# A graph network's front: edge windows gathered in node order, ranking before the table, places kept on chip

## The chip, the cores and the metric

The kernel runs on one NeuronCore of a Trainium2 chip. The metric is the device time of one execution in microseconds, the median over several runs. A separate execution is profiled; its times count from the start of its span.

The engines are TensorE (PE, with its weight loads PEld), VectorE (DVE), ScalarE (ACT), GpSimd (POOL) and SyncE (SP). Each works through its own instructions in order. SP and ACT issue plain transfers; POOL issues the indirect ones, which gather or scatter rows by an index list.

## The reference

The graph has 1250 nodes with 768 features and 20,000 edges, sorted by destination. Two layers follow each other, each behind a layer norm and ReLU and each with a residual. The first consists of two attention convolutions, with 8 heads and then 1:

```python
fs = (x @ Ws + bs).reshape(-1, H, D)
fd = (x @ Wd + bd).reshape(-1, H, D)
e = leaky_relu(fs[src] + fd[dst], 0.2)
logits = einsum('ehd,hd->eh', e, attn)
alpha = softmax of logits over the edges of each dst
out = elu(segment_sum(alpha[:, :, None] * fs[src], dst))
```

The second is a relational convolution, where each of 34 edge types has a 768x768 matrix that multiplies the mean of a node's neighbours of that type, and then a plain graph convolution.

## The kernel before, in words

All inputs and outputs are float32. The nodes are ranked by degree and cut into ten tiles of 128, so that each tile has a fixed number of edge slots (33, 22, 20, ... 11: `CAPS`, 179 in all). One slot of a tile is one "row" of the attention: one indirect gather of 128 source rows.

`fast_front` prepares this.

- It loads the edges and the nodes, normalizes the nodes (stored as `h0_d`) and transposes them to `hT` on TensorE.
- `sources(j)` (L802 on) multiplies node tile j by the first layer's source weights: two accumulations of twelve products and a bias product, two copies on ACT, and one store to the table `fs_d` on SP. There are ten such tiles.
- The ranking counts on VectorE how many 32-edge rows start below a node (L768), gathers one row of 32 destinations for each node (`got`, L775) and so finds where its edges begin (`first`, L827) and its degree. A product with a shifted identity (`sh_ps`, L830) brings each partition the first edge of the next. The degrees are broadcast as keys by eight products (L857, L858), and ten counts (L863) give the ranks. Ten scatters (L878) write records of four integers (node, first edge, degree) to the DRAM table `rank_d` at the node's rank, and one load (`rk`, L899) brings them back in rank order.
- The lists follow in rank order. `win_d` holds each edge packed as type * 2048 + source, in overlapping windows of 64. Ten gathers (`win`, L910) fetch each node's window, and five steps of three VectorE instructions (L924 to L927) shift it by its offset. `f.ell` is the result; `f.srci` (L929) is the source index that the attention gathers by.
- `pairs()` (called later, from `prepare_lists`) gives each edge a place in the lists of the second layer: counts of each type (L957, L959), masks (L965), prefix products on TensorE (L968 to L977), then the turns (L1025 to L1028), the arithmetic on the prefix sums (L984 to L1014), the picks (L1022, L1023) and the places (L1066). A product (`fl_ps`, L1061) raises a flag where the graph does not fit.

`attention` then runs over the rows. `front` gathers a row into a ring of 24 buffers and computes its logits in three VectorE instructions (L1205, L1210, L1211). `back` scales it by the softmax on ACT (L1263) and sums on TensorE (L1265), which frees its buffer. Tiles are cut in chunks: the first tile's are 16 and 17 rows long, and the back of one chunk runs beside the front of the next. `negated1` gathers a tile's own nodes (`h0`) and multiplies them for the destination term `nfd` (L1409). `finish1` ends a tile with two more matrix products and scatters its row of the second table.

Behind the gathers of the first attention, `list_edges` issues the scatters that write each edge to its place in `pair_d` (L1149), one for each row of edges, 179 in all. A `rate` of 0.9 scatters is due for each gathered row from row 20 of the first tile; at the last row 60 more are due, which empties the list. They need the places and the filled `pair_d` (L1363).

The order of the work: each engine's order is fixed by a planner that traces the program, estimates times, and takes among the instructions that are ready the one that stands first in the program. `tc.issue_after(x)` puts what a block issues on x's engine behind x. In the kernel before this sets TensorE's order: tile 0, the shift product, tile 1, the key products, tile 2; the other seven tiles follow in program order. Buffers of pools that are closed are reused by later pools, which wait for their last readers: the attention's gather buffers lie where the front's `hT` and weights were.

Of the kernel before, what the change touches and what calls it, by code (L numbers as in the profile page):

```python
# [10 lines left out]
F32 = mybir.dt.float32  # L11
# [614 lines left out]
def fast_front(ctx, tc, f, x, src, dst, edge_type, W1s, b1s, W1d, b1d, attn1, attno, W_rel):  # L626
# [34 lines left out]
    rank_d = dram.tile([NP, 4], I32, name="f_rank_d")  # L661
# [9 lines left out]
    f.ell = keepp.tile([P, NT, S0], I32, name="f_ell")  # L671
# [3 lines left out]
    f.place_d = dram.tile([P, NT * S0], I32, name="f_place_d")  # L675
    f.w1d = keepp.tile([P, KC, D], F32, name="f_w1d")

    with ExitStack() as front:
# [141 lines left out]
        last = sources(0)  # L820
# [8 lines left out]
        with tc.issue_after(last.ins):  # L829
            last = nc.tensor.matmul(sh_ps[:, 0:1], shift, first[:, 0:1], start=True, stop=True)  # L830
        with tc.issue_after(last.ins):
            last = sources(1)
# [3 lines left out]


# [14 lines left out]
        with tc.issue_after(last.ins):  # L852
            for g in range(2):
                wide = ps_m.tile([P, 2, 512], F32, name="wide", tag="ag").rearrange("p a b -> p (a b)")
                for lo, hi in ((0, 512), (512, N // 2)):
                    at = slice(g * (N // 2) + lo, g * (N // 2) + hi)
                    nc.tensor.matmul(wide[:, lo:hi], ones16[:EP], flat2[:, at], start=True, stop=False)  # L857
                    last = nc.tensor.matmul(wide[:, lo:hi], big16[:EP], flat[:, at], start=False, stop=True)  # L858
                nc.scalar.copy(keys[:, g * (N // 2):(g + 1) * (N // 2)], wide[:, :N // 2])
# [7 lines left out]
        rec = prep.tile([P, NT, 4], I32, name="rec")  # L867
        nc.vector.memset(rec, 0)
        nc.vector.tensor_copy(rec[:, :, 0], node)
        nc.vector.tensor_copy(rec[:, :, 1], first[:, :NT])  # L870
        nc.vector.tensor_copy(rec[:, :, 2], deg)

        past = prep.tile([NP - N, 4], I32, name="past")
# [10 lines left out]
        with tc.issue_after(last_keys.ins):  # L884
            sources(2)


        packed = prep.tile([EP, EC], I32, name="packed")
        nc.vector.scalar_tensor_tensor(packed, ev[:, 2, :], 2048.0, ev[:, 0, :], op0=ALU.mult, op1=ALU.add)
        zrow = prep.tile([1, RW], I32, name="zrow")  # L890
        nc.vector.memset(zrow, 0)
        pk = packed.rearrange("p (r c) -> p r c", c=RW)
        nc.scalar.dma_start(win_d[1:NR + 1, :RW].rearrange("(p r) c -> p r c", p=EP), pk)
        nc.scalar.dma_start(win_d[0:NR, RW:].rearrange("(p r) c -> p r c", p=EP), pk)
        nc.scalar.dma_start(win_d[NR:NR + 1, RW:], zrow)


        rk = prep.tile([P, NT, 4], I32, name="rk")
# [3 lines left out]
        nc.vector.tensor_copy(f.degf, rk[:, :, 2])  # L902
        arow = prep.tile([P, NT], I32, name="arow")
        nc.vector.tensor_scalar(arow, rk[:, :, 1], 5, None, op0=ALU.arith_shift_right)
        nc.vector.tensor_scalar(arow, arow, float(NR - 1), 1.0, op0=ALU.min, op1=ALU.add)
        offs = prep.tile([P, NT], I32, name="offs")
        nc.vector.tensor_scalar(offs, rk[:, :, 1], RW - 1, None, op0=ALU.bitwise_and)
        win = prep.tile([P, NT, WIN], I32, name="win")
        for k in range(NT):
            nc.gpsimd.indirect_dma_start(  # L910
                out=win[:, k, :], out_offset=None, in_=win_d[:, :],
                in_offset=bass.IndirectOffsetOnAxis(ap=arow[:, k:k + 1], axis=0))
        wf = prep.tile([P, NT, WIN], F32, name="wf")
        nc.vector.tensor_copy(wf, win)
        bits = prep.tile([P, 5, NT], F32, name="bits")
        for i in range(5):
            bi = prep.tile([P, NT], I32, name="bi", tag="bi", bufs=2)
            nc.vector.tensor_scalar(bi, offs, i, 1, op0=ALU.arith_shift_right, op1=ALU.bitwise_and)
            nc.vector.tensor_copy(bits[:, i, :], bi)
        for i in (4, 3, 2, 1, 0):  # L920
            b = 1 << i
            L = S0 + b - 1
            df = prep.tile([P, NT, S0 + 15], F32, name="df", tag="df")
            nc.vector.tensor_sub(df[:, :, :L], wf[:, :, b:b + L], wf[:, :, :L])  # L924
            nc.vector.tensor_tensor(df[:, :, :L], df[:, :, :L],
                                    bits[:, i, :, None].to_broadcast([P, NT, L]), op=ALU.mult)
            nc.vector.tensor_add(wf[:, :, :L], wf[:, :, :L], df[:, :, :L])  # L927
        nc.vector.tensor_copy(f.ell, wf[:, :, :S0])
        nc.vector.tensor_scalar(f.srci, f.ell, 2047, None, op0=ALU.bitwise_and)  # L929
# [5 lines left out]
        def pairs():  # L935
# [13 lines left out]
            typ = pp.tile([P, NT, S0], I32, name="typ")  # L949
            nc.vector.tensor_scalar(typ, f.ell, 11, None, op0=ALU.arith_shift_right)  # L950
            tv = pp.tile([P, NT, S0], F16, name="tv")
            nc.vector.scalar_tensor_tensor(tv, pad, 100.0, typ, op0=ALU.mult, op1=ALU.add)
# [101 lines left out]
            pl_i = pp.tile([P, NT, S0], I32, name="pl_i")  # L1054
# [11 lines left out]
            nc.vector.scalar_tensor_tensor(pl_i, pad, float(P * COLS), pl, op0=ALU.mult, op1=ALU.add)  # L1066
            nc.sync.dma_start(f.place_d[:, :], pl_i.rearrange("p k s -> p (k s)"))

        for j in range(3, NT):
            sources(j)  # L1070
# [53 lines left out]
def fast_rest(ctx, tc, f, x, src, dst, edge_type, W1s, b1s, W1d, b1d, attn1, ln1_w, ln1_b,  # L1124
# [44 lines left out]
    def attention(H, table, negated, attn_e, first, loads, finish, rate, rest):  # L1169
# [21 lines left out]
        def front(c, i):  # L1191

            t, s = c.t, c.first + i
            fs = pool.tile([P, RW], F32, name="fs", tag="fs", bufs=ring)
            row = gather(fs[:, :W], table[:, :], f.srci[:, t.k, s:s + 1])
            fs = fs[:, :W].rearrange("p (h e) -> p h e", h=H)
            if s >= CHUNK or t.k:
                list_edges(row, rate)
            if t.k == NT - 1 and s == t.S - 1:
                list_edges(row, rest)  # L1200
            if t.lg is None:
                lg = pool.tile([P, S0 * f.H], F32, name="lg", tag="lg", bufs=2)
                t.lg = lg[:, :S0 * H].rearrange("p (s h) -> p s h", h=H)
            z = rows_tile("z", 2)
            nc.vector.tensor_tensor(z, fs, t.nfd, op=ALU.max)  # L1205
            if H == 1:
                nc.vector.scalar_tensor_tensor(z[:, 0, :], z[:, 0, :], 1.0, attn_e[:, 0, :], op0=ALU.mult,  # L1207
                                               op1=ALU.mult, accum_out=t.lg[:, s, :])
            else:
                nc.vector.tensor_mul(z, z, attn_e)  # L1210
                nc.vector.tensor_reduce(t.lg[:, s, :], z, axis=AX.X, op=ALU.add)  # L1211
            c.rows.append(fs)
# [133 lines left out]
    def prepare_lists():  # L1346
# [22 lines left out]
        f.place = rp.tile([P, NT, S0], I32, name="place")  # L1369
        nc.sync.dma_start(f.place, f.place_d.rearrange("p (k s) -> p k s", k=NT))  # L1370
# [19 lines left out]
    with ExitStack() as one:  # L1390
# [46 lines left out]
        attention(H, f.fs_d, negated1, f.attn_1, prepare_lists, loads1, finish1, 0.9, 60)  # L1437
# [277 lines left out]
```

## Time and profile before

| | us |
|---|---|
| median of 3 runs | 2816.5 (2815.39 to 2821.32) |
| the profiled execution | 2810.31 |
| its span | 2808.5 |
| TensorE busy | 2396.5 (85%) |
| VectorE busy | 1615.1 (58%) |
| GpSimd busy | 1471.1 (52%) |
| ScalarE busy | 852.6 (30%) |

The front lasts until about 147 us (table complete). The first attention's gathers begin at 152 and its tail ends at 902. The second attention begins there, and from about 1260 TensorE's products for the 34 types dominate, until 2567. The last part sums over neighbours.

A busy time is an average over stages; what counts in a stage is the wait that ends last there. In a line of groups, the count stands after the x, then the busy time and the mean length in ns, then the idle time before the group and what ended it. In a line of the timeline the start and the length come first, and idle time before it stands in brackets with its releaser.

### The profile page before, as it was taken

To read this page: it belongs to the slowest core of one execution; us is meant where nothing else is said; L and a number is where in the kernel's file an instruction comes from. 1 tells how busy PE (TensorE), PEld (TensorE's weight loads), DVE (VectorE), ACT (ScalarE), POOL (GpSimd) and SP (SyncE) were. 2 spreads that over 40 slices of the span, in tenths; PEclk is the share of its full clock that TensorE was granted. 3 is DMA by queue.
4 is the path that set the end of the run, shared out by engine and by line. 5 is a ranking of instruction groups with operands and counts; after the bars stand their busy time and mean duration, and the time that the engine had idled before them with its cause. 6 is when DMAs were issued, how large, how long until landed. Compare 5 with 4: busy or idle time off the path is not lost. (4 is left out here: it accounts for less than half of the span.)

```text
span 2808.5 us, 24226 instructions
## 1 busy us (share of the span) xinstructions
PE 2396.5 (85%) x7859; PEld 1395.3 (50%) x7859; DVE 1615.1 (58%) x2382; ACT 852.6 (30%) x2340; POOL 1471.1 (52%) x1039
## 2 busy tenths in 40 slices
PE   6942684789898386889599999999999999997998
PEld 3521252445454243545366666666666666664455
DVE  5579979898994999999463433343333333310000
ACT  3003774776762122333212122212212212221000
POOL 1332877787884776776374555455455544421000
PEclk9976997999999698999799999999999999999999
DMA  6144443444431766675477777777677777665211
GB/s 213 46 157 156 134 132 91 125 145 134 133 97 53 277 206 189 212 220 169 169 196 214 191 185 197 184 187 186 181 201 186 184 201 198 174 147 136 75 45 51
DMA packets 130769, 447.82 MB, mean 159 GB/s; under 512 B 25016, under 2 KB 27601, under 8 KB 130634
## 3 DMA queue, kind: packets, MB, share of 16 engines
q0 software_dynamic: 77792, 305.26, 41.7%
q1 hardware_dynamic: 48041, 133.96, 13.4%
q10 hardware_dynamic: 4800, 6.96, 0.7%
q8 instruction: 65, 1.06, 0.2%
q14 instruction: 71, 0.57, 0.1%
HBM read 357.08 MB, written 89.11 MB: 159 GB/s over the span
## 5 line engine op out<-in xcount | busy, mean ns | idle before, releaser
L1114 PE MATMUL ps<-wrel,mT 128*128 128x384 f32 x3336 | 1099.4, 486 | 1.2 <-DMA wrel<-in_L_gnn_W_rel_dram 1.2
L1114 PEld LDWEIGHTS ps<-wrel,mT 128*128 128x128 f32 x3336 | 623.2, 190 | 407.4 <-issue 1.5
L1145 POOL DMA_INDIRECT g<-r_h_d,lists x241 | 365.9, 1518 | 474.1 <-DVE g L1566 302.3
L1265 PE MATMUL ag<-fs,identf 128*128 128x384 f32 x716 | 290.2, 539 | 173.2 <-ACT fs L1263 163.4
L1263 ACT ACTIVATE fs<-fs,lg 128x96 f32<-128x96 f32 x1376 | 370.6, 362 | 2.4 <-issue 1.9
L1566 DVE TENSOR_TENSOR g<-g,g 128x768 f32<-128x768 f32 x68 | 64.6, 949 | 526.4 <-DMA g<-r_h_d,lists 464.7
L1205 DVE TENSOR_TENSOR z<-fs,nfd 128x776 f32<-128x776 f32 (+1 forms) x358 | 344.0, 976 | 39.6 <-DMA fs<-f_fs_d,srci 22.6
L1255 PE MATMUL ag<-fs,dg 128*128 128x384 f32 x716 | 252.3, 514 | 86.2 <-ACT dg L1253 45.9
L1145 POOL DMA_INDIRECT fs<-f_fs_d,srci x179 | 245.9, 1374 | 103.1 <-issue 47.2
L1592 POOL DMA_INDIRECT r_h_d<-y,lists x139 | 227.3, 1635 | 133.1 <-ACT y L1591 65.8
L1149 POOL DMA_INDIRECT r_pair_d<-rec,place x179 | 240.9, 1346 | 101.3 <-DVE lg L1211 48.6
L1265 PEld LDWEIGHTS ag<-fs,identf 128*128 128x128 f32 x716 | 135.2, 204 | 315.7 <-ACT fs L1263 247.5
L1145 POOL DMA_INDIRECT fs<-r_fs_d,srci x179 | 242.5, 1355 | 82.6 <-PE ag L1255 35.5
L1506 DVE SCALAR_TENSOR_TENSOR arow<-node,from_f,arow 128x1250 f16<-128x1250 f16 x179 | 270.7, 1514 | 3.7
L1255 PEld LDWEIGHTS ag<-fs,dg 128*128 128x128 f32 x716 | 142.9, 202 | 190.8 <-ACT dg L1253 91.1
L1591 ACT COPY y<-ps 128x768 f32<-128x768 f32 x71 | 56.8, 799 | 482.0 <-PE ps L1114 482.0
L1589 ACT ACTIVATE y<-ps,rcnt 128x768 f32<-128x768 f32 x68 | 61.3, 902 | 444.4 <-PE ps L1114 444.4
L1207 DVE SCALAR_TENSOR_TENSOR z<-z,attn_o 128x769 f32<-128x769 f32 x179 | 180.2, 1027 | 0.0
L1210 DVE TENSOR_TENSOR z<-z,attn 128x776 f32<-128x776 f32 x179 | 168.3, 954 | 0.1
L1211 DVE TENSOR_REDUCE lg<-z 128x8 f32<-128x776 f32 x179 | 167.9, 950 | 0.1
L1647 DVE COPY gT<-hb 128x512 f32<-128x512 f32 (+1 forms) x9 | 5.4, 603 | 250.0 <-ACT gT L1646 250.0
L1643 PE MATMUL hb<-adj,h 125*128 125x512 f32 (+1 forms) x360 | 130.9, 526 | 14.6 <-DMA h<-r_h_d 14.6
(274 smaller groups left out, 2269.7 us busy)
## 6 DMA issues: line engine op xcount, KB each, us to landing
wrel<-in_L_gnn_W_rel_dram SPq DMA_DIRECT2D x37, 2304.0 KB
g<-r_h_d,lists POOLq DMA_INDIRECT x241
r_nfd_d<-fd SPq DMA_DIRECT2D x10, 384.0 KB
nfd<-r_nfd_d SPq DMA_DIRECT2D x10, 384.0 KB
r_x_d<-xb SPq DMA_DIRECT2D x10, 384.0 KB
x1r<-r_x_d SPq DMA_DIRECT2D x10, 384.0 KB
f_fs_d<-o_s SPq DMA_DIRECT2D x9, 388.0 KB
x<-in_x_dram SPq DMA_DIRECT2D x9, 384.0 KB
```

Source lines behind the costliest of these rows:

```text
L1114: last = nc.tensor.matmul(ps[:n, half, :f.HW], hT[:, k, j * P:j * P + n], w[:, k, cols], start=(k == 0), stop=(k == f.KC - 1 and not bias))
L1145: return nc.gpsimd.indirect_dma_start(out=to, out_offset=None, in_=table, in_offset=bass.IndirectOffsetOnAxis(ap=idx, axis=0))
L1149: s = nc.gpsimd.indirect_dma_start(out=table, out_offset=bass.IndirectOffsetOnAxis(ap=idx, axis=0), in_=rows, in_offset=None, **kw)
L1205: nc.vector.tensor_tensor(z, fs, t.nfd, op=ALU.max)
L1207: nc.vector.scalar_tensor_tensor(z[:, 0, :], z[:, 0, :], 1.0, attn_e[:, 0, :], op0=ALU.mult, op1=ALU.mult, accum_out=t.lg[:, s, :])
L1210: nc.vector.tensor_mul(z, z, attn_e)
L1211: nc.vector.tensor_reduce(t.lg[:, s, :], z, axis=AX.X, op=ALU.add)
L1255: nc.tensor.matmul(c.ps[:, half, :HW], dg, fs[:, 0, half * HW:(half + 1) * HW], start=begin, stop=end)
L1263: nc.scalar.activation(fs[:, h, :HD], fs[:, h, :HD], AF.Copy, scale=t.lg[:, s, h:h + 1])
L1265: nc.tensor.matmul(c.ps[:, half, :HW].rearrange("p (h d) -> p h d", d=HD), f.identf, fs[:, half * H // 2:(half + 1) * H // 2, :HD], start= ...
L1506: nc.vector.scalar_tensor_tensor(a, node16, from_f[:, k, s:s + 1], a, op0=ALU.is_equal, op1=ALU.add)
L1592: s = nc.gpsimd.indirect_dma_start(out=h1_d[:, :], out_offset=bass.IndirectOffsetOnAxis(ap=j.node, axis=0), in_=y, in_offset=None, compute ...
```

## The change

The edge windows are gathered and shifted in node order, before the ranks exist, and the scatter to ranks carries the finished slots. Its records have 35 integers (node, degree, 33 slots) instead of four. After the reload only the two fields are separated, source and type; the type is kept (`f.typ`) and the packed slots (`f.ell`) are not.

All ten table tiles follow the key products on TensorE; the shift product and the key products wait for no table tile.

The places are computed into a buffer that stays, where before they were stored to DRAM and loaded again.

The edge scatters are due differently: none before row 23 of the first tile, 32 (40 times the rate) at that row, then 0.8 a row; what remains is due at the last row as before.

```diff
-    rank_d = dram.tile([NP, 4], I32, name="f_rank_d")
+    rank_d = dram.tile([NP, 2 + S0], I32, name="f_rank_d")
...
-    f.ell = keepp.tile([P, NT, S0], I32, name="f_ell")
+    f.typ = keepp.tile([P, NT, S0], I32, name="f_typ")
...
-    f.place_d = dram.tile([P, NT * S0], I32, name="f_place_d")
+    f.place = keepp.tile([P, NT, S0], I32, name="place")
...
-        last = sources(0)
...
-        with tc.issue_after(last.ins):
-            last = nc.tensor.matmul(sh_ps[:, 0:1], shift, first[:, 0:1], start=True, stop=True)
-        with tc.issue_after(last.ins):
-            last = sources(1)
+        nc.tensor.matmul(sh_ps[:, 0:1], shift, first[:, 0:1], start=True, stop=True)
...
+        packed = prep.tile([EP, EC], I32, name="packed")
+        nc.vector.scalar_tensor_tensor(packed, ev[:, 2, :], 2048.0, ev[:, 0, :], op0=ALU.mult, op1=ALU.add)
...
+        nc.scalar.dma_start(win_d[1:NR + 1, :RW].rearrange("(p r) c -> p r c", p=EP), pk)
+        nc.scalar.dma_start(win_d[0:NR, RW:].rearrange("(p r) c -> p r c", p=EP), pk)
...
+        nc.vector.tensor_copy(begin, first[:, :NT])
+        nc.vector.tensor_scalar(arow, begin, 5, None, op0=ALU.arith_shift_right)
...
+        for j in range(NT):
+            nc.gpsimd.indirect_dma_start(
+                out=win[:EP, j, :], out_offset=None, in_=win_d[:, :],
+                in_offset=bass.IndirectOffsetOnAxis(ap=arow[:EP, j:j + 1], axis=0))
...
-        with tc.issue_after(last.ins):
-            for g in range(2):
...
+        for g in range(2):
+            wide = ps_m.tile([P, 2, 512], F32, name="wide", tag="ag").rearrange("p a b -> p (a b)")
+            for lo, hi in ((0, 512), (512, N // 2)):
...
+        wf = prep.tile([P, NT, WIN], F32, name="wf")
+        nc.vector.tensor_copy(wf[:EP], win[:EP])
...
+        for i in (4, 3, 2, 1, 0):
+            b = 1 << i
+            L = S0 + b - 1
...
+            nc.vector.tensor_sub(df[:EP, :, :L], wf[:EP, :, b:b + L], wf[:EP, :, :L])
+            nc.vector.tensor_tensor(df[:EP, :, :L], df[:EP, :, :L],
+                                    bits[:EP, i, :, None].to_broadcast([EP, NT, L]), op=ALU.mult)
+            nc.vector.tensor_add(wf[:EP, :, :L], wf[:EP, :, :L], df[:EP, :, :L])
+        rec = prep.tile([P, NT, 2 + S0], I32, name="rec")
         nc.vector.tensor_copy(rec[:, :, 0], node)
-        nc.vector.tensor_copy(rec[:, :, 1], first[:, :NT])
-        nc.vector.tensor_copy(rec[:, :, 2], deg)
+        nc.vector.tensor_copy(rec[:, :, 1], deg)
+        nc.vector.tensor_copy(rec[:EP, :, 2:], wf[:EP, :, :S0])
...
         with tc.issue_after(last_keys.ins):
-            sources(2)
+            sources(0)
...
-        for k in range(NT):
-            nc.gpsimd.indirect_dma_start(
-                out=win[:, k, :], out_offset=None, in_=win_d[:, :],
-                in_offset=bass.IndirectOffsetOnAxis(ap=arow[:, k:k + 1], axis=0))
...
-        nc.vector.tensor_copy(f.ell, wf[:, :, :S0])
-        nc.vector.tensor_scalar(f.srci, f.ell, 2047, None, op0=ALU.bitwise_and)
+        nc.vector.tensor_copy(f.degf, rk[:, :, 1])
+        nc.vector.tensor_scalar(f.srci, rk[:, :, 2:], 2047, None, op0=ALU.bitwise_and)
+        nc.vector.tensor_scalar(f.typ, rk[:, :, 2:], 11, None, op0=ALU.arith_shift_right)
...
-            nc.vector.scalar_tensor_tensor(pl_i, pad, float(P * COLS), pl, op0=ALU.mult, op1=ALU.add)
-            nc.sync.dma_start(f.place_d[:, :], pl_i.rearrange("p k s -> p (k s)"))
-
-        for j in range(3, NT):
+            nc.vector.scalar_tensor_tensor(f.place, pad, float(P * COLS), pl, op0=ALU.mult, op1=ALU.add)
+
+        for j in range(1, NT):
             sources(j)
...
-            if s >= CHUNK or t.k:
+            if t.k == 0 and s == ring - 1:
+                list_edges(row, 40 * rate)
+            elif t.k or s >= ring:
                 list_edges(row, rate)
...
-        f.place = rp.tile([P, NT, S0], I32, name="place")
-        nc.sync.dma_start(f.place, f.place_d.rearrange("p (k s) -> p k s", k=NT))
...
-        attention(H, f.fs_d, negated1, f.attn_1, prepare_lists, loads1, finish1, 0.9, 60)
+        attention(H, f.fs_d, negated1, f.attn_1, prepare_lists, loads1, finish1, 0.8, 60)
```

## The prediction

> **What bounds the kernel now.** I read the page first (how the span divides), then busy time by stage, then the timeline of the first 280 us, then the waits of VectorE and GpSimd. The page's own line and its two telling groups:
>
> ```profile
> span 2808.5 us, 24226 instructions
> L1114 PE MATMUL ps<-wrel,mT 128*128 128x384 f32 x3336 | 1099.4, 486 | 1.2 <-DMA wrel<-in_L_gnn_W_rel_dram 1.2
> ...
> L1149 POOL DMA_INDIRECT r_pair_d<-rec,place x179 | 240.9, 1346 | 101.3 <-DVE lg L1211 48.6
> ```
>
> From 1260 us on TensorE's products set the pace (1.2 us of waiting in 1099), and nothing there is edited: that part only moves as a whole with the end of the first attention layer, at 902. By stage up to there (engines in the order PE, weight loads, DVE, ACT, POOL, then clock, DMA share, GB/s):
>
> ```profile
> 41.00:147.00 106.00, 101.51 (x284) 49.71 (x284) 56.01 (x128) 9.12 (x20) 24.77 (x23) 0.97 0.16 51
> ...
> 164.00:188.00 24.00, 9.51 (x25) 5.37 (x25) 10.54 (x34) 0.48 (x1) 17.25 (x18) 0.61 0.88 305
> 188.00:226.00 38.00, 11.49 (x34) 6.41 (x32) 37.83 (x47) 0.86 (x2) 0.00 (x0) 0.70 0.02 9
> 226.00:263.00 37.00, 2.80 (x5) 1.50 (x6) 36.90 (x53) 5.62 (x18) 3.58 (x3) 0.50 0.71 261
> 263.00:812.00 549.00, 433.22 (x1251) 229.66 (x1249) 489.78 (x675) 382.38 (x1331) 427.26 (x309) 0.91 0.45 128
> ```
>
> TensorE is full to 147 (the table). VectorE is full from 188 to 263. From 263 to 812 POOL is busy 427 us, and its 309 instructions each have 0.3 us of issue before them: 520 of 549. VectorE has 490. Both bind there, close together. The timeline of the front (start, length, engine, line):
>
> ```profile
> 100.86 0.37 SPq L899 DMA_DIRECT2D rk<-f_rank_d  x1
> 128.03 0.33 DVE L929 TENSOR_SCALAR srci<-f_ell 128x330 int32<-128x330 int32 x1
> 145.77 0.76 DVE L965 TENSOR_SCALAR mask<-cnt 128x340 bf16<-128x340 f32 x3
> 146.24 0.89 PE L812 MATMUL ps<-bias,ones_row 1*98 1x388 f32 x2
> 151.81 0.95 POOL L1145 DMA_INDIRECT h<-f_h_d,f_permg  x1 [35.31 <-ACT tot L979]
> ...
> 187.19 1.33 DVE L1022 TENSOR_TENSOR pick<-same,pdf 128x1122 f32<-128x1122 f16 x1 [0.88 <-DVE pdf L1014]
> 225.46 0.48 DVE L1066 SCALAR_TENSOR_TENSOR pl_i<-pad,pl 128x330 int32<-128x330 f32 x1
> 228.10 0.32 SPq L1370 DMA_DIRECT2D place<-f_place_d  x1
> 233.52 1.62 POOL L1149 DMA_INDIRECT r_pair_d<-rec,place  x1 [47.09 <-DVE lg L1211]
> ...
> 263.40 3.35 POOL L1145 DMA_INDIRECT fs<-f_fs_d,srci  x1 [25.69 <-PE ag L1265]
> 272.79 1.83 DVE L1205 TENSOR_TENSOR z<-fs,nfd 128x776 f32<-128x776 f32 x2
> ```
>
> The reader should see that the lists (128) and the table (147) come close together, that the first gather (151.8) waits for the table, not the lists, and that POOL idles 47 us before the first place and 26 more before the 25th row. The last view is VectorE's waits between 186 and 905:
>
> ```profile
> DVE z L1205 <- DMA fs<-f_fs_d,srci: 22.6, 18, 4.2
> DVE nfd L1409 <- PE ag L1265: 21.8, 3, 12.1
> ```
>
> Cut by 40 us, the first comes as 16.4 us between 460 and 660 and none later: where POOL binds VectorE, it does so up to about row 132 of 179.
>
> **The ranking chain.** `first` is ready at 50.1. Its product now waits behind a table tile until 56.2; then it would run at once. From that product's result to the second diagonal are 2.15 us of VectorE (56.61 to 58.76), so 52.8; the eight key products took 1.7, with a cold clock some 0.4 more: 54.9; key copies 55.3. Ten rank counts of 1.56: 71.0 (before 84.4). The ten window gathers (1.25 apart, 2.7 to land) run from 51 to 66 on a POOL that now idles from 45 to 85, hidden by the counts. Masking (9.4) and packing the record (0.6) then precede the scatters: 81.0. Ten scatters at 1.48, 2.6 to the reload on SP's queue (table stores behind it leave as it does, as now at 101.3), 2.5 for it, two masks: 101.4, against 128.4. Wider rows (140 bytes for 16) have no row here: between no cost and a doubling of the ten scatters, 15 us. I take 0, because what follows hides it: VectorE then does 17.7 us of counts (to 119) and 16 us of turns (to 135) and stands until the table is done at about 157. If the cover went, each us above 20 would count.
>
> **The table.** Tile 0 leaves the time from 35 to 56, where it ran between transposes and waited for the column sums of the weights; the transposes end at 40 either way. TensorE takes 9.9 us a tile, ten tiles 99. Begun at 54.9, with 1.0 for the cold clock (the half tile at 49.4 took 5.9 for 4.95), it ends at 154.9, 7.8 later. The three sets of prefix products come after it again: in the present order VectorE did all turns before anything made of `tot`, so when the order was planned the masks had long been ready and the table tiles, earlier in the program, still went first. The first gather, behind the last table store, moves to 159.6.
>
> **From the table to the picks.** Now the last totals are ready 7.0 after the table, but VectorE is in its turns until 162.1; the last totals are used at 168.98 and the first pick runs at 187.19, 18.2 later. Afterwards the turns are done, so 161.9 and 180.1: 7.1 earlier. Gathers now end at 186.4, before the picks; afterwards they run to 193.5, beside four picks. VectorE stood 13.4 us before about 19 instructions among those gathers, 0.7 each: 2.8 back. Bounds 0 and 7.1. VectorE's shift: 4.3 earlier.
>
> **Places and the burst.** No trip of the places through DRAM: from L1066's end (225.9) to the fill 2.6 us saved; the SP queue loses two DMAs, and nothing queued there is late. The first list scatter moves from 233.5 to 226.6. Then 32 scatters stand ahead of the gather of row 24 on POOL, which now issues at 263.4 and is used at 272.8. Price p of one: at least 1.27 (0.97 and 0.30 of issue); at most 2.35 (17 POOL instructions in the 40 us from 420, VectorE full). Nearest are the three at 233.5 to 237.7, 1.50 each, and the 40 back to back from 813 to 873, 1.49. With 1.5, row 24 issues at 274.6, 11.2 late, lands 4 later at 278.6, and VectorE, wanting it at 268.5, stands 10.1. Behind the burst wait the gathers of rows 24 on; VectorE waits for them, ACT and TensorE for VectorE.
>
> **The lower rate.** 0.8 instead of 0.9 scatters a row, at 1.39 and 0.30, gives 0.169 us a row: over 106 rows (24 to 130) 17.9. POOL's lateness of 11.2 becomes 6.7 of lead, and VectorE, 5.8 late after its stand, can follow it, since 12.5 of its 16.4 us of gather waits would have to go. Bounds: none goes, or all 16.4. At the end 23 scatters remain instead of 36; L1426 at 875.84 came 1.07 after its product: 1.0.
>
> Sum: 11.2 - 17.9 - 1.0 = -7.7. The profiled execution took 2810.31, so 2802.6; the median of the runs is 6.2 above it: 2816.5 - 7.7 = 2808.8, taken as 2809.
>
> **A rule beside this.** At 273.59 a gather took 3.65 us while VectorE ran two pairs of two-input instructions of 1.83. The Trainium skill, SBUF — State Buffer, section Who interferes with whom, says that such an instruction and a GpSimd instruction that reads SBUF block each other whole, whoever issues first. Were every burst scatter to meet one pair, 1.27 + 1.83 = 3.1 each would make the sum +43.5 instead of -7.7; the three at 233.5 ran among single such instructions for 1.5, so I use that.
>
> **Rivals.** (a) The prefix products slip between table tiles. For: the masks are ready at 119. Against: the order argued above. Then the lists finish near 170, rows start at 176 (gather 159.6, 3.9 landing, 12 of products), row 24 is wanted at 244, 29 earlier, and the burst ends at 240: about -30, 2786. (b) The burst costs more. Net is 226.6 + 32p - 263.4 - 17.9 - 1.0 = 32p - 55.7: from p = 1.74 it is a loss. For: VectorE is full there. At 2.35 it gives +19.5; with the scatters after VectorE stops at 1.27, +4; midway +12, 2829. (c) The picks gain nothing, or the relieved gather waits come back as waits for TensorE (21.8 already): 0 to +5, 2819.
>
> **How the numbers follow.** Mine 0.48, (a) 0.17, (b) 0.27, (c) 0.08. A measurement tells 0.2%, 5.6 us. Mine by itself spans p = 1.27 (-15) to no relief (+5): 2801 to 2821, seven tenths faster, two the same. Faster: 0.17 + 0.34 = 0.51; slower: most of (b), half of (c), a tenth of mine: 0.32; same 0.17. The range 2784 to 2834 reaches just past (a), and to (b) at its dear end but one; outside lie two in ten.
>
> **What would show it.** Right: key products near 53, `srci` near 101, the last table product near 155, first gather near 160, first list scatter near 227, then 32 together, the gather of row 24 near 275, VectorE waiting there about 10, and few gather waits after 460. Wrong: prefix products before 150; the burst over by 262 (better than I say) or after 282; a list chain over 135; the order from the table on changed, so that rows or picks swap places.

## The result and the profile after

Over 20 executions each, the changed kernel took 2811.5 us in the median (2803.3 to 2818.5) and the kernel before 2817.6 (2809.8 to 2828.4). The ratio of after to before is 0.9976, 95% interval 0.9967 to 0.9986: 0.24% faster. The prediction was 2809.0 against a before of 2816.5, a ratio of 0.9973. The profiled executions took 2808.86 and 2810.31.

That agreement is better than the reasons behind it, as the rest shows. First the same views as before the change. The page:

```profile
span 2807.1 us, 24226 instructions
...
L1107 PE MATMUL ps<-wrel,mT 128*128 128x384 f32 x3336 | 1099.9, 486 | 1.3 <-DMA wrel<-in_L_gnn_W_rel_dram 1.3
...
L1142 POOL DMA_INDIRECT r_pair_d<-rec,place x179 | 266.6, 1489 | 67.2 <-issue 49.4
```

The relational products are as they were (1.3 us of waiting in 1099.9). The list scatters got dearer, 1489 ns in the mean instead of 1346, and GpSimd's idle time before them fell from 101.3 to 67.2. Busy time by stage (columns PE, weight loads, DVE, ACT, POOL, clock, DMA share, GB/s):

```profile
41.00:147.00 106.00, 94.59 (x263) 47.54 (x263) 68.62 (x160) 8.53 (x19) 27.86 (x23) 0.91 0.15 48
164.00:188.00 24.00, 11.42 (x34) 6.30 (x31) 23.45 (x38) 1.15 (x3) 18.82 (x18) 0.71 0.86 276
188.00:226.00 38.00, 11.36 (x30) 6.56 (x30) 37.90 (x56) 2.24 (x3) 21.13 (x15) 0.63 0.63 200
226.00:263.00 37.00, 16.35 (x34) 6.84 (x34) 32.86 (x42) 19.22 (x73) 32.13 (x17) 0.66 0.40 152
263.00:812.00 549.00, 423.59 (x1225) 223.95 (x1225) 481.20 (x664) 371.59 (x1286) 418.48 (x305) 0.89 0.46 129
```

From 164 to 188 VectorE is now full (23.45 of 24, before 10.54). From 226 to 263 GpSimd has 32.13 us of work where it had 3.58. The timeline (start, length, engine, line, what it waited for):

```profile
53.51 0.59 PE L876 MATMUL wide<-diag,big 125*128 125x512 f16 x1 [2.51 <-DVE diag L867]
102.55 0.37 SPq L921 DMA_DIRECT2D rk<-f_rank_d  x1
105.74 0.33 DVE L925 TENSOR_SCALAR srci<-rk 128x330 int32<-128x330 int32 x1
155.60 0.89 PE L812 MATMUL ps<-bias,ones_row 1*98 1x388 f32 x2
158.65 0.18 DVE L995 TENSOR_SCALAR more<-tot 128x34 f32<-128x34 f32 x1 [17.50 <-ACT tot L974]
161.20 0.99 POOL L1138 DMA_INDIRECT h<-f_h_d,f_permg  x1 [60.29 <-DVE f_xrel L1039]
171.42 1.33 DVE L1017 TENSOR_TENSOR pick<-same,pdf 128x1122 f32<-128x1122 f16 x1
209.68 0.49 DVE L1060 SCALAR_TENSOR_TENSOR place<-pad,pl 128x330 int32<-128x330 f32 x1
215.81 1.81 POOL L1142 DMA_INDIRECT r_pair_d<-rec,place  x1 [12.91 <-DMA r_pair_d<-fill]
275.35 0.99 POOL L1138 DMA_INDIRECT fs<-f_fs_d,srci  x1 [0.31 <-issue]
279.28 0.97 DVE L1200 TENSOR_TENSOR z<-fs,nfd 128x776 f32<-128x776 f32 x1 [20.42 <-DMA fs<-f_fs_d,srci]
```

Two lines carry the story. At 158.65 VectorE has stood 17.5 us for the totals, which come behind the last table product (155.60, before 146.24). At 279.28 it has stood 20.4 us for the row whose gather waited behind 32 scatters. Between the two it was 15.8 us ahead of the kernel before (first pick 171.42 against 187.19, places 209.68 against 225.46); behind the second it is 5.6 us late: the reduction of that row, row 24, ends at 283.7 where it ended at 278.1. (The line at 272.79 before the change holds two rows; row 24 is the second.) VectorE's waits between 186 and 905:

```profile
DVE z L1200 <- DMA fs<-f_fs_d,srci: 41.3, 19, 20.4
DVE fs L1419 <- PE ps L1107: 18.7, 2, 9.4
DVE nfd L1402 <- PE ag L1260: 16.1, 2, 9.3
```

Without the one stand of 20.4 the waits for gathers are 20.9, against 22.6 before. They hardly fell. The first gather of the second attention is 4.0 earlier (901.9 against 905.9), its last one 5.0 (1299.5 against 1304.5).

In what follows, "row 24" is the end of VectorE's reduction of the 25th row, and "the stretch" the time from there to the same instruction of the last row, 178; both are read from the one profiled execution of each kernel. Before: 278.1 and 566.1. After: 283.7 and 557.3. The e-numbers name the kernels of the experiments.

### The profile page after: what moved, and what is told of

The parts are those of the page before. It is cut to its first block, busy times and chain, and to the rows that moved or that the text cites. A ratio compares the mean times of both kernels' runs of the same rounds, so it can differ in the third digit from the quotient of the medians.

```text
span 2807.1 us, 24226 instructions
## 1 busy us (share of the span) xinstructions
PE 2398.0 (85%) x7859; PEld 1395.6 (50%) x7859; DVE 1614.5 (58%) x2381; ACT 853.3 (30%) x2340; POOL 1489.4 (53%) x1039
## 3 DMA queue, kind: packets, MB, share of 16 engines
q1 hardware_dynamic: 47753, 133.78, 13.4%
## 5 line engine op out<-in xcount | busy, mean ns | idle before, releaser
L1107 PE MATMUL ps<-wrel,mT 128*128 128x384 f32 x3336 | 1099.9, 486 | 1.3 <-DMA wrel<-in_L_gnn_W_rel_dram 1.3
L1260 PE MATMUL ag<-fs,identf 128*128 128x384 f32 x716 | 291.1, 540 | 156.5 <-ACT fs L1258 123.7
L1142 POOL DMA_INDIRECT r_pair_d<-rec,place x179 | 266.6, 1489 | 67.2 <-issue 49.4
L1138 POOL DMA_INDIRECT fs<-f_fs_d,srci x179 | 237.7, 1328 | 86.4 <-issue 49.8
L1582 ACT ACTIVATE y<-ps,rcnt 128x768 f32<-128x768 f32 x68 | 61.3, 902 | 444.9 <-PE ps L1107 444.9
```

The costliest lines, as they stand in the source:

```text
L1107: last = nc.tensor.matmul(ps[:n, half, :f.HW], hT[:, k, j * P:j * P + n], w[:, k, cols], start=(k == 0), stop=(k == f.KC - 1 and not bias))
L1138: return nc.gpsimd.indirect_dma_start(out=to, out_offset=None, in_=table, in_offset=bass.IndirectOffsetOnAxis(ap=idx, axis=0))
L1142: s = nc.gpsimd.indirect_dma_start(out=table, out_offset=bass.IndirectOffsetOnAxis(ap=idx, axis=0), in_=rows, in_offset=None, **kw)
L1260: nc.tensor.matmul(c.ps[:, half, :HW].rearrange("p (h d) -> p h d", d=HD), f.identf, fs[:, half * H // 2:(half + 1) * H // 2, :HD], start= ...
```

## The experiments

**The front without the new spread of the scatters (e1).**

```diff
-            if t.k == 0 and s == ring - 1:
-                list_edges(row, 40 * rate)
-            elif t.k or s >= ring:
+            if s >= CHUNK or t.k:
                 list_edges(row, rate)
...
-        attention(H, f.fs_d, negated1, f.attn_1, prepare_lists, loads1, finish1, 0.8, 60)
+        attention(H, f.fs_d, negated1, f.attn_1, prepare_lists, loads1, finish1, 0.9, 60)
```

> The kernel after with the list scatters spread as before (from row 20 on, 0.9 to a row), so only the front, the order of TensorE and the places are new. Theory (the front brings VectorE 15.6 us ahead, the 32 scatters ahead of the gather of row 24 cost 20.4 of it there): first pick near 171 as in the kernel after, the gather of row 24 near 249, no long stand of VectorE at row 24, its row near 257 instead of 272.8 before and 279.3 after; the end 8 to 16 us before the kernel before, 2802 to 2810. Rival (the 6 us come from the lower rate and the front's lead is swallowed by later waits): 2814 to 2818, with longer waits for TensorE's products and for gathers between 280 and 420.

Measured: 2804.5 us, ratio to before 0.9968 (0.9956 to 0.998). First pick at 170.1, row 24 at 262.6 (15.5 ahead of before), no stand. GpSimd was idle when row 24's gather could go:

```profile
247.93 1.60 POOL L1138 DMA_INDIRECT fs<-f_fs_d,srci  x1 [28.33 <-PE ag L1258]
```

It waited 28.3 us for TensorE to free the slot; 28 us are open there for scatters, not 60. The theory held. Of the 15.5 us, 9.5 are left at the last row.

**The new spread without the front (e2).** The edit is e1's, the other way round, on the kernel before.

> The kernel before with the new spread of the list scatters alone (32 ahead of the gather of row 24, then 0.8 to a row). Theory: the burst starts at 233.5 and takes 32 of 1.5 to 1.86, so the gather of row 24 issues at 282 to 293 instead of 263.4, VectorE stands 14 to 24 us there, and 6 to 9 of it come back in later waits: 2823 to 2833. Rival (the gain comes from the lower rate): 2808 to 2814.

Measured: 2816.3 us, 1.0017 (1.0002 to 1.0032): slower, but less than I expected. The gather of row 24 issued at 283.6, so the 32 took 1.57 each; the stand was 14.1; row 24 came at 292.1, 14.0 late. The stretch was 556.1 instead of 566.1, which gave 10 of the 14 back. So the rival was wrong that the new spread brings the gain, and I was wrong on how much of the loss survives.

**Fewer and more scatters in one place (e3, e4).**

```diff
-                list_edges(row, 40 * rate)
+                list_edges(row, 20 * rate)
```

and `80 * rate` in e4.

> The kernel after with 16 scatters ahead of the gather of row 24 instead of 32; the 16 left over fall to the end of the first attention (39 there instead of 23). Theory: at 1.86 each from 215.8 the 16 are through by 246, before the first products free the slot of row 24 (near 249), so VectorE hardly stands there (20.4 in the kernel after), row 24 is near 259, and of the 20 us between 6 and 16 reach the end: 2796 to 2806. Rival (what is lost or won at row 24 is made up by later waits, so the stand costs nothing): 2809 to 2813.

> The kernel after with 64 scatters ahead of the gather of row 24 instead of 32: the suspected cost doubled. Theory: the 32 more run mostly while VectorE stands, at 1.27 to 1.5 each, so the stand grows by 41 to 48 to 61 to 68 us, none of the 64 later rows is short of POOL, and the end is 33 to 46 later than the kernel after: 2844 to 2857. Rival (later waits make it up, because POOL has 32 fewer behind it): under 2825.

Measured: 16 scatters 2800.8 us, 0.995 (0.9934 to 0.9967); 64 scatters 2860.9 us, 1.0159 (1.0133 to 1.0185). With 16, VectorE stood 2.6 us for a gather in the whole time up to 290, and row 24 came at 269.5, although this execution's table ended at 162.4 instead of 156.5. With 64 the stand was 61.3, row 24 came 40.9 later than in the kernel after, and the last row 52.2 later: nothing came back. The theory for e4 undershot (2844 to 2857). The scatters ahead of row 24 are on the path as soon as they outlast the wait for the slot. In e1 the fourth product of TensorE's sums freed it. The gather of row 24 issued 2.2 us after that product with 16 scatters (256.7), 27.1 after it with 32, and 67.9 after it with 64.

**Places through DRAM again (e5).**

```diff
+            pl_i = pp.tile([P, NT, S0], I32, name="pl_i")
-            nc.vector.scalar_tensor_tensor(f.place, pad, float(P * COLS), pl, op0=ALU.mult, op1=ALU.add)
+            nc.vector.scalar_tensor_tensor(pl_i, pad, float(P * COLS), pl, op0=ALU.mult, op1=ALU.add)
+            nc.sync.dma_start(f.place_d[:, :], pl_i.rearrange("p k s -> p (k s)"))
...
+        f.place = rp.tile([P, NT, S0], I32, name="place")
+        nc.sync.dma_start(f.place, f.place_d.rearrange("p (k s) -> p k s", k=NT))
```

> The kernel after with the places written to DRAM and read back, as before. Theory (the burst is on the path, so what comes ahead of it counts whole): first list scatter at 218.4 instead of 215.8, 2.6 later, the gather of row 24 near 278 instead of 275.4, VectorE's stand there 23 instead of 20.4, and the rows after it 2 to 3 later. Rival (the trip hides): gather of row 24 and the stand within 0.5 of the kernel after. The time itself can't tell 2 or 3 us.

Both were wrong. The first scatter came at 216.65, only 0.8 later, since in the kernel after it waits for the fill of the lists (12.91 in the line at 215.81), not for the places. And the burst was shorter: the gather of row 24 at 267.2 instead of 275.4, the stand 14.0 instead of 20.4. One execution took 2802.6 us. The trace says why. The kernel after, GpSimd and VectorE in the burst:

```profile
229.25 0.97 POOL L1142 DMA_INDIRECT r_pair_d<-rec,place  x1 [0.30 <-issue]
229.76 1.82 DVE L1200 TENSOR_TENSOR z<-fs,nfd 128x776 f32<-128x776 f32 x2
230.53 3.66 POOL L1142 DMA_INDIRECT r_pair_d<-rec,place  x1 [0.31 <-issue]
231.51 1.83 DVE L1205 TENSOR_TENSOR z<-z,attn 128x776 f32<-128x776 f32 x2
233.26 1.81 DVE L1206 TENSOR_REDUCE lg<-z 128x8 f32<-128x776 f32 x2
```

The same place with the places through DRAM:

```profile
224.04 0.97 POOL L1144 DMA_INDIRECT r_pair_d<-rec,place  x1 [0.30 <-issue]
224.56 0.95 DVE L1207 TENSOR_TENSOR z<-z,attn 128x776 f32<-128x776 f32 x1
...
225.32 1.04 POOL L1144 DMA_INDIRECT r_pair_d<-rec,place  x1 [0.30 <-issue]
225.44 0.96 DVE L1202 TENSOR_TENSOR z<-fs,nfd 128x776 f32<-128x776 f32 x1
226.31 0.95 DVE L1208 TENSOR_REDUCE lg<-z 128x8 f32<-128x776 f32 x1
```

In the kernel after VectorE runs its rows here in pairs: two maxima, two products, two reductions. The four two-input instructions stand back to back for 3.6 us, and the scatter that begins in the first of them takes 3.66; two scatters pass per 5.25 us. With the places through DRAM the rows interleave: one row's product, the next row's maximum, then a reduction. The scatters take 0.97 and 1.04, and four pass in the same time.

The order of the instructions does not settle the price, though. Both kernels meet pairs and pay alike for them: three scatters of 3.66 in the kernel after, and 3.56, 3.95 and 3.66 in e5, whose pairs come later. And from 245 on the kernel after interleaves its rows in the very same order, at 2.31 to 2.61 a scatter:

```profile
250.04 0.95 DVE L1205 TENSOR_TENSOR z<-z,attn 128x776 f32<-128x776 f32 x1
250.40 2.31 POOL L1142 DMA_INDIRECT r_pair_d<-rec,place  x1 [0.30 <-issue]
250.92 0.95 DVE L1200 TENSOR_TENSOR z<-fs,nfd 128x776 f32<-128x776 f32 x1
251.79 0.95 DVE L1206 TENSOR_REDUCE lg<-z 128x8 f32<-128x776 f32 x1
```

This scatter begins 0.36 us into a product and ends 0.9 us into the reduction; in e5 the scatter at 225.32 begins 0.12 us before its product gives way to the maximum, and is not held. In the rows outside the pairs lies the difference between the two bursts, 59.5 and 50.6 us. All kernels with 32 scatters beside working rows agree: the dear ones, 1.86 a scatter (after) and 1.78 (e7), have six of 2.0 to 2.6 us, and the cheap ones, 1.57 (e2, e11) and 1.58 (e5), have none. So the price seems to go with the point in a row's instructions at which a scatter begins. No rule for it is shown: the scatter at 230.53, among the pairs, also begins 0.1 us before its maximum gives way to the next, and is held. What sets that point was not tried.

**GpSimd's load (e7).**

```diff
-                list_edges(row, 40 * rate)
+                list_edges(row, 80 * rate)
...
-        attention(H, f.fs_d, negated1, f.attn_1, prepare_lists, loads1, finish1, 0.8, 60)
+        attention(H, f.fs_d, negated1, f.attn_1, prepare_lists, loads1, finish1, 0.4, 130)
```

> The kernel after with the burst of 32 kept, but 0.4 scatters to a row behind it instead of 0.8, the rest (about 85 instead of 23) at the end of the first attention. It takes another 0.68 us a row from GpSimd. Reason A (the prediction's: GpSimd's load makes VectorE's waits for gathers): the waits for gathers from row 24 to row 178, 20.7 in the kernel after, fall under 7, and that stretch (556.5 us) is 12 to 20 shorter. Reason B (those waits come with a slot that TensorE frees late or with the copying beside other work, and GpSimd idles 15 to 30 us in each of these stretches): they stay over 12, and the stretch is within 8 of 556.5. The end is 60 to 95 later by the tail in both.

Measured (one execution, 2851.9 us): the stretch fell from 557.3 to 542.3 and the waits for gathers from 20.7 to 10.8. Between my two reasons: GpSimd's load does hold VectorE, but 62 scatters fewer bought 15.0 us, 0.24 each, where each takes GpSimd about 1.7. The end came 40 us after that of the kernel after, not the 60 to 95 I had expected. The kernels of the study, ordered by rate, point the same way. At 0.9 a row (before, e1, e10, e13) the stretch is 566 to 575, mean 570.1; at 0.8 (after, e2 to e6, e8, e11, e12) 555 to 569, mean 559.7. That is 10.4 us. The waits for gathers in it are 3.3 shorter (23.8 to 20.5 in the mean), those of `nfd` for TensorE's products 8.5 (26.4 to 17.9). It is not only that a late row 24 is caught up: with row 24 at 252 to 256 the stretch is 566.8 and 575.4 at 0.9 (e13, e10) and 561.0 at 0.8 (e12). Nor is it the number of scatters alone: e4 has 26 fewer in the stretch than the kernel after, and its stretch is 11.4 longer.

**Prefix products ahead of the last two table tiles (e6), and with 16 scatters (e8).** This is my rival (a), made on purpose:

```diff
-        for j in range(1, NT):
+        for j in range(1, 8):
             sources(j)
-        rows_only.close()
         ranking.close()
         pp = front.enter_context(tc.tile_pool(name="f_pp", bufs=1, side="right"))
-        f.pairs, f.front = pairs, front.pop_all()
+        pairs()
+        rows_only.close()
+        f.front = front.pop_all()
...
+            with tc.issue_after(last.ins):
+                for j in range(8, NT):
+                    sources(j)
```

The last three lines stand in `pairs` behind the last total; `last` is its product.

> The kernel after with the three sets of prefix products ahead of the last two table tiles instead of behind all ten; the last table product comes 7 later, near 163. Theory: VectorE, which stands from 141.2 to 158.7 in the kernel after, goes on near 144; first pick near 156 instead of 171.4; the rows still wait for the table, so row 0 ends near 191 (185.7 after), places are ready near 187 to 195 instead of 210, the burst ends near 258 to 262, the gather of row 24 goes there instead of 275.4, VectorE's stand at row 24 falls from 20 to 8 to 12, row 24 is 14 to 17 earlier, and the end 8 to 16 earlier than the kernel after: 2794 to 2803. Rival (the later table costs what the earlier lists bring, because rows can't start before the table): 2804 to 2812.

> Both candidates at once: prefix products ahead of the last two table tiles, and 16 instead of 32 scatters ahead of the gather of row 24. Theory (both gains are on the path of VectorE): no stand at row 24, row 24 near 253 (283.7 after, 269.5 and 262.6 in the runs without the burst of 32), the end 12 to 22 before the kernel after, 2788 to 2799. Rival (with no stand left, the earlier lists bring nothing because rows start by the table): the same as with 16 scatters alone, 2799 to 2804.

Measured: e6 2817.5 us, 1.0015 (1.0 to 1.0029), row 24 at 290.6; e8 2804.3 us, 0.9969 (0.9956 to 0.9982), row 24 at 272.3 and a wait of 19.6 at the softmax. In e6 the first pick came at 151.4 and the places at 175.4, earlier even than the theory wanted, and still both times lie above their ranges: there was no gain over the kernel after (e6) or over 16 scatters alone (e8). VectorE's stand had moved to the first softmax. The longest wait of ScalarE in e6 between 180 and 290 (line, what it waited for, us in total, times, longest), and the timeline there:

```profile
ACT hT L1101 <- PE pt L1099: 96.1, 1, 96.1
```

```profile
264.09 1.00 POOL L1142 DMA_INDIRECT h<-f_h_d,f_permg  x1 [0.30 <-issue]
268.25 1.51 PE L1099 MATMUL pt<-identf,h 128*128 128x128 f32 x6 [86.37 <-DMA h<-f_h_d,f_permg]
269.21 1.06 ACT L1101 COPY hT<-pt 128x384 f32<-128x384 f32 x2 [96.11 <-PE pt L1099]
271.93 0.39 DVE L1230 TENSOR_REDUCE den<-lg 128x8 f32<-128x128 f32 x1 [40.09 <-ACT lg L1228]
```

The planner had put the gather of the second tile's `h` behind the 32 scatters. ScalarE's copy of its transposes comes ahead of the first softmax's exponential in ScalarE's order, so the exponential, and VectorE behind it, waited for a gather that nobody needed yet. In the kernel after, this gather issues at 200 to 202, ahead of the burst, probably because the places come later there.

**Two ways out of that (e10, e12).** e10 is e6 with the scatters spread as in e1. e12 is e8 with the second tile begun earlier:

```diff
             if i == chunks[0].n // 2:
                 begin(1)
+                begin(2)
```

> Prefix products ahead of the last two table tiles, with the list scatters spread as before the change (from row 20 on, 0.9 to a row): no 32 or 16 at one place. Theory (in the runs with the prefix products ahead, VectorE's 40.1 and 19.6 us at the first softmax are ScalarE, held by the copies of tile 1's transposes, because tile 1's gather of h stands behind the burst on GpSimd): the gather of h comes near 220, VectorE's wait at the softmax is under 6, row 24 ends near 252 to 257 (262.6 with the old spread alone), and the end is 4 to 9 us before that kernel: 2796 to 2801 against a before of 2814. Rival (the table 7 us later takes back what the earlier lists bring): 2802 to 2807.

> Prefix products ahead of the last two table tiles, 16 scatters ahead of the gather of row 24, and the second tile's h asked for in the loop of the first chunk, so that its gather stands ahead of the burst. Theory as in the run before: VectorE's 19.6 us at the first softmax fall under 3, the burst is through near 246, row 24 ends near 254 to 258 (272.3 with the gather of h behind the 16, 269.5 with 16 scatters and no move of the prefix products), and the end is 10 to 16 before the kernel with the gather behind: 2788 to 2795. Rival (ScalarE is held by something else, or the wait only moves to row 24): 2800 to 2806.

Measured: e10 2798.6 us, 0.9937 (0.9914 to 0.9961), row 24 at 255.6; e12 2793.1 us, 0.9934 (0.991 to 0.9957), row 24 at 254.4 and no wait at the softmax. Both theories held, with the first `h` gather of the second tile at 179.7 in e12. e12 is the fastest kernel of the study by its median, ahead of both given ones; its interval overlaps those of e10, e13 and e3.

**The old order of TensorE (e13).** The front of the change and the old spread, with the table's first two tiles back around the products of the ranking:

```diff
+        last = sources(0)
...
-        nc.tensor.matmul(sh_ps[:, 0:1], shift, first[:, 0:1], start=True, stop=True)
+        with tc.issue_after(last.ins):
+            last = nc.tensor.matmul(sh_ps[:, 0:1], shift, first[:, 0:1], start=True, stop=True)
+        with tc.issue_after(last.ins):
+            last = sources(1)
...
-        for g in range(2):
+        with tc.issue_after(last.ins):
+            for g in range(2):
...
-            sources(0)
+            sources(2)
...
-        for j in range(1, NT):
+        for j in range(3, NT):
```

> One part undone: the front of the change with the lists spread as before (run e1), but TensorE in the old order, the first two table tiles around the products of the ranking. Theory (the order only moves VectorE's stand: in the kernel after it is done with the turns at 141 and waits 17.5 us for a table that the new order ends 8 us later): the lists come 10 to 15 later than in e1 (sources of the rows near 116 to 121 instead of 105.7), the last table product near 147 as before, first gather near 152 instead of 160.3, VectorE stands under 5 us ahead of the places' arithmetic, first pick between 164 and 171 (170.1 in e1) if that arithmetic runs without gaps and near 180 if it stands as it did in the kernel before, row 24 within 252 to 263 in the first case, and the end no later than e1: 2796 to 2805 against a before of 2814. Rival (the new order of TensorE brings the gain): first pick after 175 without gaps, the end 2807 to 2814.

Measured: 2796.4 us, 0.9953 (0.9933 to 0.9973), against 0.9968 for the same kernel with the new order. Its timeline:

```profile
145.39 0.89 PE L812 MATMUL ps<-bias,ones_row 1*98 1x388 f32 x2
148.44 0.18 DVE L1000 TENSOR_SCALAR more<-tot 128x34 f32<-128x34 f32 x1 [2.18 <-ACT tot L979]
150.98 1.17 POOL L1143 DMA_INDIRECT h<-f_h_d,f_permg  x1 [44.71 <-DVE hit L1039]
160.58 1.33 DVE L1022 TENSOR_TENSOR pick<-same,pdf 128x1122 f32<-128x1122 f16 x1
```

The sources of the rows come 4.1 later than in e1 (110.8 and 106.7; I had expected 10 to 15), the table ends 9.3 earlier (146.3 and 155.6), and VectorE stands 2.2 us for it where the kernel after stands 17.5. The first pick is 9.5 earlier than in e1, row 24 at 252.4 instead of 262.6. On the path to row 24 the reordering of TensorE is a loss: it brings forward lists that then wait for the table that it delays. The two intervals of the times overlap, so the time alone doesn't show this. The traces do, though with some luck in the size: the profiled execution of e13 was 9.3 us under its median, that of e1 1.9 above.

**Why the arithmetic ahead of the picks ran through (e11).** In the kernel before, this arithmetic stood 13.4 us among the gathers, ahead of 15 instructions; in the kernel after it ran beside gathers too, and stood 1.4. Three instructions in the kernel before, then the same three after:

```profile
182.30 0.51 DVE L1009 TENSOR_TENSOR pdf<-pdf,xcol 128x340 f32<-128x340 f32 x1 [3.20 <-remote]
183.69 0.51 DVE L1010 TENSOR_TENSOR pdf<-pdf,q_i 128x340 f32<-128x340 f32 x1 [0.88 <-DVE pdf L1009]
185.09 0.52 DVE L1013 TENSOR_TENSOR pdf<-pdf,tcol 128x340 f32<-128x340 f32 x1 [0.89 <-issue]
```

```profile
169.16 0.51 DVE L1004 TENSOR_TENSOR pdf<-pdf,xcol 128x340 f32<-128x340 f32 x1
169.71 0.51 DVE L1005 TENSOR_TENSOR pdf<-pdf,q_i 128x340 f32<-128x340 f32 x1
170.26 0.58 DVE L1008 TENSOR_TENSOR pdf<-pdf,tcol 128x340 f32<-128x340 f32 x1
```

The edit delays it, so that the gathers have run longer when it comes:

```diff
+            for i in range(20):
+                nc.vector.tensor_tensor(pre[0], pre[0], pre[0], op=ALU.max)
             for i in range(2):
                 nc.vector.tensor_sub(pre[i], pre[i], pre[i + 1])
```

> The kernel after with 20 more two-input instructions of VectorE (a tile of 340 numbers against itself, about 0.51 each as the ones behind them, 8.6 to 11 us in all) between the prefix products and the arithmetic of the places; the values stay the same. It asks why this arithmetic stood 13.4 us in the kernel before and hardly in the kernel after, both beside the gathers of the first rows. Reason C (it stands where the gathers have been running some 5 to 10 us before it): first pick later by 15 or more, at 187 or later, with over 5 us of gaps among the instructions from 169 on. Reason D (it does not hang on how long the gathers have run): first pick at 180 to 183, gaps under 2.5.

Measured: first pick 180.3, gaps 1.5. So it is not the time since the gathers began. In every kernel with the new front in which gathers ran beside it the arithmetic ran through, in both with the old front it stood (13.4 and 12.8). What decides it stays open.

## Why the prediction was right or wrong

**Key products, lists.** Right: 53.5 (predicted near 53). The sources of the rows came at 105.7, not 101.4, because the planner ran the masking between the rank counts and VectorE stood 6.6 us for the windows; as argued, this cost nothing, since VectorE then stood anyway. The wider records cost nothing either: their ten scatters went 1.49 us apart, 1.48 foretold.

**The table and its prefix products.** Right in place, and in size within 2 us: the last table product ended at 156.5 (154.9), the prefix products came behind it, the first gather at 161.2 (159.6). But I took the later table as a given and never asked what the front would be worth without it. e13 answers: 10 us at row 24.

**From the table to the picks: the step that failed.** I had the first pick 7.1 earlier and VectorE's shift 4.3, by carrying over the 18.2 us from the last totals to the first pick, with the 13.4 us of standing in them, and then charging 2.8 more for gathers beside picks. The pick came 15.8 earlier, and all of it held up to the places. With the arithmetic running through, the way from the last totals (used at 164.3) to the first pick took 7.1 us instead of 18.2; from the first total it took 12.8 instead of 24.8. Beside the picks VectorE did not stand, and some gathers took 2.0 to 2.5 us. Why the arithmetic ran through stays open (e11).

**Places and the burst.** I had the first scatter at 226.6, 32 at 1.5, and the gather of row 24 at 274.6. It issued at 275.4, by two errors that cancel: the start was 10.8 earlier (215.8) and 32 x 0.36 = 11.5 went to the price of 1.86. VectorE, 15 us ahead and not 4, then stood 20.4 and not 10.1, and was 5.6 late at row 24, as against 5.8: the same two errors cancelled here too, and that is luck. The places' 2.6 us were no saving: the fill of the lists is what the first scatter waits for. As to the rule weighed there, the Trainium skill, SBUF — State Buffer, section Who interferes with whom, has reductions free of contention and two-input instructions not. The 3.66 of a scatter that begins among four two-input instructions in a row, and ends 0.9 us into the reductions, agrees with it. That VectorE is blocked in turn does not show here: its instructions kept their 0.95 us beside the burst. The whole block for every scatter, 3.1 each, was too dear, and the 1.5 of the nearest rows too cheap: scatters of 0.97 and of 2.0 to 3.7 us lie side by side, and what parts them stays open.

**The lower rate.** The direction was right, the place not. I wanted 12.5 of 16.4 us of gather waits to go between rows 24 and about 130; the waits over the whole stretch went from 22.3 to 20.7. The stretch is 8.8 us shorter nevertheless, 10.4 by the comparison of rates above, and most of that is a shorter wait of `nfd` for TensorE. GpSimd, with 38 of the 557 us free of work and issue, was close to full, and still it did not set the pace alone: taking 62 scatters away, about 105 us of its time, bought 15.0 (e7). Why fewer scatters shorten VectorE's waits for TensorE was not tried.

**The sum and the rivals.** 11.2 - 17.9 - 1.0 = -7.7 stood against -6.1 in the medians. Row 24 was 5.6 late and the last row 3.1 early; the tail brought 0.9 more (1.0 foretold), so that the second attention began 4.0 earlier, and the profiled execution ended 1.4 earlier. The traces thus show about half of the -7.7, because the stretch gave 8.8 and not 17.9; that the medians came as near to it as -6.1 is partly luck. Rival (b)'s form, a loss from 1.74 a scatter, fails with its start of 226.6: at 1.86 there was no loss, because the burst began 10.8 sooner. Rival (a) was not what happened. Made on purpose, it brought the first pick to 151, 36 us ahead of the kernel before, and nothing at the end until the gather of `h` no longer stood behind the burst (e10, e12); my 2786 for it left out the wait that comes next.

By parts, at row 24: the lists in node order with places on chip 25.7 earlier (e13), TensorE's order 10.2 back (e1), the new spread 21.1 back (after). Up to the last row the stretch then returned 8.8 against the kernel before, and 14.7 against e1, which differs from the kernel after in the spread and the rate alone. Each part comes from one profiled execution of each kernel and is uncertain by some us, as the front of e3 shows (below).

## What to carry to other kernels

Before crediting a front that finishes earlier, find the one queue that everything behind it waits in, and fit the moved work into the idle time that is measured there: 16 scatters ahead of row 24 cost no stand, 32 cost 14 to 20 us. When a wait is removed, list what stands behind it in the in-order queues of the other engines: here a gather nobody needed yet held ScalarE, and through it VectorE, for 40 us. A prediction whose total comes out right deserves the same check of its terms, since two here were off by 11 us in opposite directions.

## What the runs showed of the hardware

- The same 32 scatters beside the same rows cost 1.57 to 1.86 us each. One that begins among four two-input instructions of VectorE in a row took up to 3.96. Beside rows in which a reduction follows every two of them, a scatter took 0.97 to 1.04 in some kernels (e2, e5, e11) and 2.3 to 2.6 in others (after, e7), with the same order of instructions.
- In two kernels (before, e2) VectorE stood 13.4 and 12.8 us, up to 3.2 at a time, in its arithmetic on 340 numbers beside gathers, and in eight others 1.0 to 1.5 us beside the same gathers. The time since the gathers began does not explain it (e11); a rule that one engine always gives way does not fit either, since beside the picks some gathers took 2.0 to 2.5 us and VectorE ran through.
- The front itself varies from execution to execution: with the same table and order the last table product ended at 154.8 to 156.5 in six profiles (after, e1, e4, e5, e7, e11) and at 162.4 in a seventh (e3), whose first gather of destinations (`got`) began at 36.9 instead of 30.4 in the kernel after, with no edit there.
